# A pre-norm transformer layer on one core: row maxima split into parts with fewer VectorE operations, value copies on ScalarE, and the value bias folded into the output bias

## The chip, the cores and the metric

The kernel runs on one core of one Trainium2 chip. The metric is the device time of one execution in microseconds (us); 1381.62 us is the median of the three runs of the kernel before (1381.47, 1381.62 and 1383.63).

## The reference

The input is x of shape (2, 2048, 256) in fp32. It goes through attention with 16 heads of 16 columns, causal, with rotary positions, and then through a gated feed-forward layer whose inputs and weights are rounded to a 4-bit grid in blocks of 16. Cut to what matters here:

```python
q = split_heads(x @ Wq.T + bq)
k = split_heads(x @ Wk.T + bk)
v = split_heads(x @ Wv.T + bv)
q, k = (rope(q), rope(k))
att = jnp.einsum('bhqd,bhkd->bhqk', q, k) / scale
att = jax.nn.softmax(jnp.where(mask, att, -jnp.inf), axis=-1)
y = jnp.einsum('bhqk,bhkd->bhqd', att, v)
return y.transpose(0, 2, 1, 3).reshape(b, t, N_EMBD) @ Wo.T + bo
...
x = x + _L0_attn_ref(_layernorm(x), ...)
x = x + _L0_ffn_ref(_layernorm(x), ...)
```

The rows of `att` sum to one, so a constant bv that is added to every row of v comes out of the attention unchanged, and `Wo` turns it into the constant row `bv @ Wo.T`, which stands beside `bo`. The drawn bv and bo are not zero.

## The kernel before

**Tiles and stages.** Each of the two sequences has 2048 rows, which are cut into four chunks of 512 (c = 0 to 3). For a chunk the kernel normalizes x, turns it on TensorE (PE) into `xnT`, and makes queries, keys and values. The values of a chunk are computed in two pairs of 128-row tiles (`values`, L1011): eight matmuls fill one PSUM bank `pv` with 2 x 256 columns, and `put` (L1027) adds the bias and lays the result out in the tile `v`, 16 columns behind one column of ones for each head (so the same product also gives the softmax's denominators). The bias comes from `bvb`, bv on all 128 partitions, which SyncE's queue (SP) fetches by a broadcast transfer (L455).

The 16 heads are treated in four groups of four; a group of a chunk is a slot, and there are 2 x 4 x 4 = 32 slots. A slot has three steps:

- `max_steps` (L1075): PE computes the scores q.k into PSUM (`sc`, L1094, two banks at a time, masked on the diagonal at L1062), and VectorE (DVE) reduces each bank to its row maxima (`reduced`, L1106; instructions at L1118). For c = 0 a row has one part and the maxima are in `mx`; for c > 0 there is one partial maximum for each block of keys, in `parts`.
- `split` (L1137): the 16 maxima of each partition are written as a sum of three bf16 numbers, because PE's transpose carries bf16. For c > 0 a reduction (L1143) first makes `mx` of `parts`. Then, twice, a bitwise AND with `UPPER` (L1156) takes the upper 16 bits as a part, and a subtraction (L1159) leaves the rest. The parts lie in the tile `mslots`, 32 places for each of 16 maxima. `turn` (L1166) transposes the upper halves of `mslots` on PE (L1175), and ScalarE (ACT) copies them to `mT` (L1179).
- `value_steps` (L1203): PE computes the scores again with the maxima subtracted by a matmul with `less` (`sx`, L1227 and L1235), ACT takes the exponential (L1250), PE multiplies with `v` (`av`, L1283), and ACT copies the sums out (L1305).

Beside this run the feed-forward layer of an earlier chunk (`ffn_steps`: `pg` L1575, `pd` L1669, turned tiles `pth` L1434; its 4-bit rounding uses GpSimd (POOL) at L593, L615, L618 and L621 and DVE at L582 to L612), the rotary steps of the next chunk on POOL (L889, L892, L919), and transfers on SP. The row `bob` (bo on all partitions, L452) is added to x by POOL (L1503) before the output projection.

**What sets the order.** The program does not run its loops in the order in which they are written. Every piece of work is given to a planner (`Plan`, `add`) with its engine, a cost in microseconds, what it reads and writes, and a due time; a list scheduler (`ordered`) plays the plan through and emits each engine's instructions in the order that results. A changed cost or engine can therefore move other instructions too. `Thing` names a piece of data or a buffer, `ROOM` tells how many buffers of a kind there are, and seven PSUM banks (`ps`) are shared by all of it. Within the first 170 planned us, where the planner sees PE idle, `kept_busy` (L484) puts idle matmuls (L488) there. Each engine works through its own instructions strictly in order.

**Names of the change.** `bqk` (L445) holds the biases of queries and keys, turned by PE from the rows `brows` (`transpose_biases`). `bvb`, `UPPER` and the tile `left` are in the kernel before only. `on_vector(n)` and `on_scalar(n)` are the planner's costs for n columns.

Of the kernel before, what the change touches and what calls it, by code (L numbers as in the profile page):

```python
# [29 lines left out]
F32 = mybir.dt.float32  # L30
# [30 lines left out]
)  # L61
MAGIC = 1.5 * 2.0**22
EXPONENT = 0x7F800000
UPPER = -0x10000

# [27 lines left out]

XIN = 3
ROOM = dict(ps=7, av=1, ex=4, qT=4, parts=4)
ROOM.update(mx=2, mparts=1, left=1, mT=2, avs=1, den=2, y=2, sums=2, over=1)
ROOM.update(xnT=1, xin=XIN, high=1, t1=1, t2=1, cs=1, dev=XIN-1)
ROOM.update(x0=1, xT=1, x1=2, xn=2, h=1, hrT=1, step=1, fdev=2, sc16=2, sc44=2, endsc16=2, endsc44=2)  # L100

# [198 lines left out]
def product(n):  # L300

    return max(n / 600, 0.17 + n / 870, 0.23) + 0.005
# [12 lines left out]
def layer_kernel(  # L315
# [123 lines left out]
    mslots = const.tile([P, TPC, GROUP, SLOT], F32, name="mslots")  # L439

    slots_of = Thing()
    bvb_, bob_ = Thing(), Thing()


    bqk = const.tile([P, 2, NBLK], F32, name="bqk")  # L445
    brows = exps.tile([2 * NBLK, P], F32, tag="ex", name="brows")
    for i, vec in enumerate((bq, bk)):
        nc.scalar.dma_start(
            brows[i * NBLK : (i + 1) * NBLK], vec.rearrange("(n o) -> n o", n=NBLK)
        )  # L450
    bvb = const.tile([P, E], F32, name="bvb")
    bob = const.tile([P, E], F32, name="bob")  # L452

    def lay_bias(tile, vec, thing, due):
        run = lambda: nc.sync.dma_start(tile, vec.partition_broadcast(P))  # L455
# [331 lines left out]
    def project_steps(b, c, blk):  # L787
# [223 lines left out]
        def values(pair, due):  # L1011
            pm = Thing("ps")

            def run(n):
                if n == 0:
                    st["pv", pair] = small(CH, "pv").rearrange("p (i o) -> p i o", i=2)
                i = 2 * pair + n
                for k in range(KE):
                    nc.tensor.matmul(  # L1019
                        st["pv", pair][:, n, :],  # L1020
                        lhsT=xnTs[b, c][:, k, i * P : (i + 1) * P],
                        rhs=wvT[:, k, :],
                        start=(k == 0),
                        stop=(k == KE - 1),
                    )

            def put():  # L1027
                nc.vector.tensor_tensor(  # L1028
                    vs[b, c][:, : TPC * N_HEAD * AUG].rearrange(
                        "p (i h e) -> p i h e", i=TPC, e=AUG  # L1030
                    )[:, 2 * pair : 2 * pair + 2, :, 1:],
                    st["pv", pair].rearrange("p i (h e) -> p i h e", e=HD),
                    bvb.rearrange("p (h e) -> p h e", e=HD)
                    .unsqueeze(1)
                    .to_broadcast([P, 2, N_HEAD, HD]),
                    ALU.add,
                )

            for n in range(2):
                add(PE, KE * product(E), lambda n=n: run(n), [xnT_[b, c], wv_], [pm], due)  # L1040
            add(DVE, 0.595, put, [pm, bvb_], [v_[b, c]], due)

        if early:
            begin.stripped = stripped
# [30 lines left out]
    def max_steps(b, c, g):  # L1075

        steps = []
        st = {}
        mx, parts = Thing("mx"), Thing("mparts")
        found = []  # L1080
        max_[b, c, g] = Thing("mT")

        def one(i, kc, d, due):
            duo = 2 * (g % 2) + d
            cols = CH if kc < c else (i + 1) * P
            ps, got = (Thing("ps"), Thing("ps")), []

            def run():
                qT = qTs[b, c, g]
                kT = kTs[b, kc, g // 2]  # L1090
                sc = [ps_s.tile([P, CH], F32, tag="ps", name="sc") for _ in range(2)]
                kept_busy(sc[0])
                for h in range(2):
                    nc.tensor.matmul(  # L1094
                        sc[h][:, :cols],
                        lhsT=strips(qT, h, d, slice(i * P, (i + 1) * P)),
                        rhs=strips(kT, h, duo, slice(0, cols)),
                        start=True,
                        stop=(kc < c),
                    )  # L1100
                if kc == c:
                    for h in range(2):
                        masked(sc, h, cols - P, mask_q)
                got.append(sc)

            def reduced(h):  # L1106
                name = "parts" if c else "mx"
                if name not in st:
                    st[name] = att.tile(
                        [P, TPC, 2, 2, NC] if c else [P, TPC, 2, 2],  # L1110
                        F32,
                        tag=name,
                        name=name,
                        bufs=1 if c else 2,
                    )
                at = st[name][:, i, h, d]
                dst = at[:, kc : kc + 1] if c else at.unsqueeze(1)
                nc.vector.tensor_reduce(dst, got[0][h][:, :cols], AX.X, ALU.max)  # L1118

            add(  # L1120
                PE,
                0.18 + 0.44e-3 * cols if kc == c else 0.27,
                run,
                [qT_[b, c, g], k_[b, kc, g // 2][g % 2], mask_q_, pick_],
                [*ps, m_order],
                due,
                [parts if c else mx],
                "strip",
                FEED_M,
                0.07,  # L1130
            )
            for h in range(2):
                own = Thing(of=parts if c else mx)
                found.append(own)
                add(DVE, on_vector(cols), lambda h=h: reduced(h), [ps[h]], [own], due)

        def split(due):  # L1137
            left = Thing("left")

            def run():  # L1140
                if c:
                    st["mx"] = att.tile([P, TPC, 2, 2], F32, tag="mx", name="mx")
                    nc.vector.tensor_reduce(  # L1143
                        st["mx"].rearrange("p i h d -> p (i h d)"),
                        st["parts"][:, :, :, :, : c + 1].rearrange(
                            "p i h d k -> p (i h d) k"
                        ),
                        AX.X,
                        ALU.max,
                    )  # L1150

                mx = st["mx"].rearrange("p i h d -> p i (h d)")
                rest = att.tile([P, TPC, GROUP], F32, tag="left", name="left", bufs=1)
                for n, (src, rest) in enumerate(((mx, rest), (rest, mslots[:, :, :, 2]))):
                    part = mslots[:, :, :, n]
                    nc.vector.tensor_scalar(  # L1156
                        part.bitcast(I32), src.bitcast(I32), UPPER, None, ALU.bitwise_and
                    )
                    nc.vector.tensor_tensor(rest, src, part, ALU.subtract)  # L1159

            if c:
                add(DVE, 1.04, run, found, [mx, left, slots_of], due - 0.1)
            else:
                add(DVE, 0.79, run, found, [left, slots_of], due - 0.1)

        def turn(due):  # L1166
            pm = Thing("ps")

            def run():

                upper = mslots.bitcast(BF16).rearrange("p i s (d two) -> p i (s d) two", two=2)
                bank = ps_s.tile([P, TPC, P], BF16, tag="ps", name="ptm")
                st["pt"] = bank
                for i in range(TPC):
                    nc.tensor.transpose(st["pt"][:, i, :], upper[:, i, :, 1], ident_b)  # L1175

            def put():
                mT = att.tile([P, CH], BF16, tag="mT", name="mT")
                nc.scalar.copy(mT, st["pt"].rearrange("p i q -> p (i q)"))  # L1179
                maxima[b, c, g] = mT  # L1180

            add(
                PE,
                0.01 + 0.08 * TPC,
                run,
                [slots_of, ident_b_],
                [pm],
                due - 0.1,
                [max_[b, c, g]],
                late=0.05,  # L1190
            )
            add(ACT, on_scalar(CH), put, [pm], [max_[b, c, g]], due - 0.1)

        for i in range(TPC):
            for kc in range(c + 1):
                for d in range(2):
                    steps.append(lambda due, i=i, kc=kc, d=d: one(i, kc, d, due))
        return steps, split, turn
# [645 lines left out]
    def transpose_biases(due):  # L1844
        pm, got = Thing("ps"), []

        def run():
            got.append(small(2 * NBLK, "ptb"))
            nc.tensor.transpose(got[0], brows, ident[: 2 * NBLK, : 2 * NBLK])

        add(PE, 0.16, run, [biases, fixed], [pm], due)
        add(
# [7 lines left out]

    begun += [(-9.88, steps[0])]
    begun += [
        (-8.6, lambda due: lay_bias(bvb, bv, bvb_, due)),
        (0.4, lambda due: lay_bias(bob, bo, bob_, due)),
        (-8.8, lay_spread),
        (-8.2, lay_mask_q),
        (-8.1, lay_pick),
# [100 lines left out]
```

## Time and profile before

| What | Value |
|---|---|
| median of three timed runs | 1381.62 us |
| span of the profiled execution (first to last instruction) | 1378.9 us |
| what the median has beyond that span | 2.7 us |
| PE busy / DVE busy | 1317.6 us (96%) / 1115.1 us (81%) |
| ACT busy / POOL busy | 749.9 us (54%) / 538.4 us (39%) |
| instructions at L1156 (AND) | 64: 13.0 + 11.1 us busy |
| instructions at L1159 (subtract) | 64: 8.6 + 9.2 us busy |
| instructions at L1028 (values plus bias, DVE) | 16: 10.7 us busy |
| mean granted TensorE clock | 0.979 of full speed |

The profiled execution is not one of the three timed ones; its own time is known as its span. Busy time is the time in which an engine had an instruction running. A busy PE is not necessarily a PE at full speed, since the ends of matmuls are modelled. The chain that ended last is followed from the last instruction back: at each step to what released it, or to the instruction before it on its engine. PEld is PE's weight load, which waits for the buffers that its matmul needs.

### The profile page before, as it was taken

The page shows a single profiled execution, that of the slowest core. Times are in us where ns is not written, and L with a number is a line of the kernel's source. Part 1 is how long each engine was busy: PE and PEld are TensorE (multiplying, and loading weights), DVE is VectorE, ACT ScalarE, POOL GpSimd, SP SyncE. Part 2 cuts the span into 40 slices and gives each one's busy share as a digit, 9 for nine tenths or more (in the row PEclk, how much of TensorE's full clock was granted, in tenths as well). Part 3 has the DMA queues.
Part 4 walks back from the last instruction along what each step waited for, and adds up shares of the span by engine and source line. Part 5 has one row for each costly group of instructions (what it writes and reads, how often), then busy time and mean ns, then how long its engine had stood idle before and what let it go on. Part 6 is the DMA issues. An engine that isn't in the chain of part 4 may idle for free.

```text
span 1378.9 us, 27730 instructions
## 1 busy us (share of the span) xinstructions
PE 1317.6 (96%) x10408; PEld 656.7 (48%) x10408; DVE 1115.1 (81%) x2415; ACT 749.9 (54%) x1670; POOL 538.4 (39%) x685
## 2 busy tenths in 40 slices
PE   7988999999999999999998999999999999999977
PEld 4544444444544444444454555444454444444445
DVE  7788989988889998875479888996878988894296
ACT  2542655556555566557643455554655566667711
POOL 4754634434423334314345644432442332320360
PEclk8998999999999999999999999999999999999988
DMA  2653432411221401221343414240130130000000
GB/s 88 133 134 100 103 94 58 104 33 55 62 41 44 107 20 41 64 45 51 89 113 94 108 44 97 66 95 22 47 86 17 43 81 13 9 9 9 9 1 19
DMA packets 61887, 84.39 MB, mean 61 GB/s; under 512 B 14772, under 2 KB 30520, under 8 KB 61752
## 3 DMA queue, kind: packets, MB, share of 16 engines
q1 hardware_dynamic: 61744, 82.61, 24.2%
q8 instruction: 82, 1.34, 0.4%
q14 instruction: 53, 0.43, 0.1%
q10 hardware_dynamic: 8, 0.00, 0.0%
HBM read 55.09 MB, written 27.49 MB: 60 GB/s over the span
## 4 chain that ended last, share of the span: by engine, by line
PE 65%; DVE 19%; POOL 5%; issue 5%; DMA 3%; ACT 2%; SPq 0%; POOLq 0%; DVEq 0%; ACTq 0%
PE av L1283 15%; PE sc L1094 9%; PE pg L1575 9%; PE sx L1227 8%; DVE parts L1118 7%; PE sx L1235 7%; PE pd L1669 6%; PE pj L837 3%; PE pth L1434 2%; PE po L1519 1%; PE pv L1019 1%; DVE scale L582 1%; DVE step L609 1%; DVE mx L1118 1%; PE sc L1062 1%
## 5 line engine op out<-in xcount | busy, mean ns | idle before, releaser
L1250 ACT ACTIVATE ex<-sx 128x512 f32<-128x512 f32 (+3 forms) x1280 | 592.8, 538 | 345.9 <-PE sx L1235 202.1
L1118 DVE TENSOR_REDUCE parts<-sc 128x1 f32<-128x512 f32 (+3 forms) x1152 | 637.9, 611 | 65.2 <-PE sc L1094 46.6
L1235 PE MATMUL sx<-qT,kT 64*128 64x512 f32 (+3 forms) x1280 | 335.6, 521 | 0.0
L1283 PE MATMUL av<-ex,v 128*32 128x512 f32 (+3 forms) x2560 | 301.3, 543 | 0.0
L1094 PE MATMUL sc<-kT,qT 64*128 64x512 f32 (+3 forms) x1280 | 280.3, 425 | 8.9 <-DMA kT<-parts 2.5
L1227 PE MATMUL sx<-mT,less 64*128 64x512 bf16 (+3 forms) x1280 | 246.5, 355 | 5.4 <-DVE parts L1118 1.6
L1094 PEld LDWEIGHTS sc<-kT,qT 64*128 64x128 f32 x1280 | 132.8, 188 | 168.1 <-DVE parts L1118 51.2
L1227 PEld LDWEIGHTS <-less 64*128 64x128 bf16 x1280 | 66.5, 94 | 213.3 <-issue 205.5
L590 POOL TENSOR_SCALAR inv<-inv 128x16 f32<-128x16 f32 (+2 forms) x82 | 17.7, 216 | 373.0 <-DVE inv L586 341.2
L1235 PEld LDWEIGHTS sx<-qT,kT 64*128 64x128 f32 x1280 | 131.3, 196 | 9.0 <-issue 6.8
L1669 PE MATMUL pd<-wdT,hrT 128*128 128x256 f32 (+1 forms) x384 | 103.9, 411 | 1.5 <-ACT hrT L1438 1.0
L1283 PEld LDWEIGHTS av<-ex,v 128*32 128x32 f32 x2560 | 52.6, 108 | 70.8 <-issue 60.4
L1669 PEld LDWEIGHTS pd<-wdT,hrT 128*128 128x128 f32 (+1 forms) x384 | 70.4, 197 | 29.1 <-issue 16.0
L889 POOL TENSOR_TENSOR t<-t,cs 128x512 f32<-128x512 f32 x31 | 39.9, 1286 | 110.2 <-DVE t L883 104.8
L1575 PE MATMUL pg<-wgT,xT 128*128 128x352 f32 x224 | 76.9, 476 | 0.9 <-ACT xT L1438 0.8
L837 PE MATMUL pj<-xnT,wqkT 128*128 128x512 f32 x128 | 73.8, 672 | 3.5 <-DVE v L1028 1.7
L1118 DVE TENSOR_REDUCE mx<-sc 128x1 f32<-128x128 f32 (+3 forms) x128 | 54.3, 477 | 25.8 <-PE sc L1062 25.8
L1575 PE MATMUL pg<-wuT,xT 128*128 128x352 f32 x224 | 74.4, 471 | 0.1
L1062 PE MATMUL sc<-pick,mask_q 64*128 64x64 bf16 x1024 | 67.3, 198 | 0.0
L615 POOL TENSOR_TENSOR h<-h,step 128x704 f32<-128x704 f32 x28 | 47.2, 1686 | 48.8 <-DVE step L612 41.0
L1601 ACT ACTIVATE h<-pg 128x352 f32<-128x352 f32 x64 | 29.9, 467 | 64.6 <-PE pg L1575 56.5
L547 POOL TENSOR_SCALAR ve<-mv 128x1 f32<-128x1 f32 x64 | 12.6, 197 | 130.4 <-DVE mv L543 127.1
(163 smaller groups left out, 1614.8 us busy)
## 6 DMA issues: line engine op xcount, KB each, us to landing
qT<-parts SPq DMA_DIRECT2D x120, 128.0 KB
kT<-parts SPq DMA_DIRECT2D x120, 128.0 KB
parts<-high SPq DMA_DIRECT2D x30, 256.0 KB
parts<-t SPq DMA_DIRECT2D x30, 256.0 KB
sums<-avs SPq DMA_DIRECT2D x28, 256.0 KB
cs<-in_rope_dram SPq DMA_DIRECT2D x8, 512.0 KB
xin<-in_L_attn_x_dram SPq DMA_DIRECT2D x28, 128.0 KB
y<-sums SPq DMA_DIRECT2D x28, 128.0 KB
```

Source lines behind the costliest of these rows:

```text
L615: queue.tensor_tensor(src(), src(), st["step"], ALU.add)
L837: nc.tensor.matmul(got["pj"], lhsT=wqkT[:, k, i, cols], rhs=xnTs[b, c][:, k, :], start=(k == 0), stop=(k == KE - 1),)
L889: (nc.gpsimd if early and i == 0 else queue).tensor_tensor(swapped, swapped, angles[b, c][:, 1, :], ALU.mult)
L1062: nc.tensor.matmul(sc[h][:, col + at : col + at + STRIP], lhsT=strips(mask, h, half), rhs=strips(pick, h), start=False, stop=(half == 1),)
L1094: nc.tensor.matmul(sc[h][:, :cols], lhsT=strips(qT, h, d, slice(i * P, (i + 1) * P)), rhs=strips(kT, h, duo, slice(0, cols)), start=True, ...
L1118: nc.vector.tensor_reduce(dst, got[0][h][:, :cols], AX.X, ALU.max)
L1227: nc.tensor.matmul(sc[h][:, off:], lhsT=strips(less[d], h), rhs=strips(mT, h, slice(off, CH)), start=True, stop=False,)
L1235: nc.tensor.matmul(sc[h][:, off:], lhsT=strips(kT, h, duo, slice(jj, jj + P)), rhs=strips(qT, h, d, slice(off, CH)), start=False, stop=(j ...
L1250: nc.scalar.activation(st[j, d][:, h, off:], got[0][h][:, off:], AF.Exp, scale=HD**-0.5)
L1283: nc.tensor.matmul(st["av"][SLOT * s : SLOT * (s + 1), off:], lhsT=v[:, at : at + SLOT], rhs=st[j, d][:, h, off:], start=(j == 0), stop=(j ...
L1575: nc.tensor.matmul(got[half], lhsT=split("xrT")[:, k, :], rhs=wT[:, k, half * IH : (half + 1) * IH], start=(k == 0), stop=(k == KE - 1),)
L1669: nc.tensor.matmul(st["pd"], lhsT=st["hrT"][:n, k, :], rhs=wdT[:n, k, :], start=(k == 0), stop=(k == KI - 1),)
```

## The change

The split loses its ANDs: each subtraction reads the upper half of the number before it directly, as a bf16 view of `mslots`. For c > 0 the reduction of `parts` writes its result straight into the first place of `mslots`; for c = 0 a copy brings `mx` there. So a split has three DVE operations (reduction or copy, subtraction, subtraction) in place of five (c > 0) or four (c = 0). `mx` (for c > 0) and `left` are gone. Values are copied by ACT from PSUM to `v` without a bias. bv comes as two more rows of `brows` on ACT's queue, is turned with bq and bk, spread by two ACT copies to `wide`, multiplied with `woT` on PE, and added to `bob` by DVE (`through_output`, due at 2.0). The broadcast transfer of bv is gone. The costs given to the planner change with these steps.

```diff
-            left = Thing("left")
+            def upper(t):
+                return t.bitcast(BF16).rearrange("p i s (d two) -> p i s d two", two=2)[
+                    :, :, :, :, 1
+                ]

             def run():
+                first, second, third = (mslots[:, :, :, n] for n in range(3))
                 if c:
-                    st["mx"] = att.tile([P, TPC, 2, 2], F32, tag="mx", name="mx")
                     nc.vector.tensor_reduce(
-                        st["mx"].rearrange("p i h d -> p (i h d)"),
+                        first,
...
-                mx = st["mx"].rearrange("p i h d -> p i (h d)")
-                rest = att.tile([P, TPC, GROUP], F32, tag="left", name="left", bufs=1)
-                for n, (src, rest) in enumerate(((mx, rest), (rest, mslots[:, :, :, 2]))):
-                    part = mslots[:, :, :, n]
-                    nc.vector.tensor_scalar(
-                        part.bitcast(I32), src.bitcast(I32), UPPER, None, ALU.bitwise_and
-                    )
-                    nc.vector.tensor_tensor(rest, src, part, ALU.subtract)
-            if c:
-                add(DVE, 1.04, run, found, [mx, left, slots_of], due - 0.1)
-            else:
-                add(DVE, 0.79, run, found, [left, slots_of], due - 0.1)
+                else:
+                    nc.vector.tensor_copy(first, st["mx"].rearrange("p i h d -> p i (h d)"))
+                high = upper(mslots)
+                nc.vector.tensor_tensor(second, first, high[:, :, :, 0], ALU.subtract)
+                nc.vector.tensor_tensor(third, second, high[:, :, :, 1], ALU.subtract)
+            add(DVE, 0.72 if c else 0.6, run, found, [slots_of], due - 0.1)
```

```diff
             def put():
-                nc.vector.tensor_tensor(
+                nc.scalar.copy(
                     vs[b, c][:, : TPC * N_HEAD * AUG].rearrange(
                         "p (i h e) -> p i h e", i=TPC, e=AUG
                     )[:, 2 * pair : 2 * pair + 2, :, 1:],
                     st["pv", pair].rearrange("p i (h e) -> p i h e", e=HD),
-                    bvb.rearrange("p (h e) -> p h e", e=HD)
...
-                    ALU.add,
                 )
-            add(DVE, 0.595, put, [pm, bvb_], [v_[b, c]], due)
+            add(ACT, on_scalar(CH), put, [pm], [v_[b, c]], due)
```

```diff
-    for i, vec in enumerate((bq, bk)):
+    for i, vec in enumerate((bq, bk, bv)):
         nc.scalar.dma_start(
...
-    bvb = const.tile([P, E], F32, name="bvb")
+    def through_output(due):
+        temp, pm, st = Thing("x1"), Thing("ps"), {}
+        def spread_out():
+            st["wide"] = ffn.tile([P, E], F32, tag="x1", name="wide", bufs=ROOM["x1"]).rearrange(
+                "p (k o) -> p k o", k=KE
+            )
+            for k in range(KE):
+                nc.scalar.copy(st["wide"][:, k, :], bqk[:, 2, k : k + 1].to_broadcast([P, P]))
+        def run():
+            st["po"] = small(E, "pbo")
+            for k in range(KE):
+                nc.tensor.matmul(
+                    st["po"],
+                    lhsT=st["wide"][:, k, :],
+                    rhs=woT[:, k, :],
...
+        def put():
+            nc.vector.tensor_tensor(bob, st["po"], bob, ALU.add)
+        add(ACT, 0.4, spread_out, [bias_], [temp], due)
+        add(PE, KE * product(E), run, [temp, wo_], [pm], due)
+        add(DVE, on_vector(E), put, [pm], [bob_], due)
...
-        (-8.6, lambda due: lay_bias(bvb, bv, bvb_, due)),
         (0.4, lambda due: lay_bias(bob, bo, bob_, due)),
+        (2.0, through_output),
```

More of the change, by code (lines that the diff above doesn't have):

```diff
@@ L63 @@
 EXPONENT = 0x7F800000
-UPPER = -0x10000
 AHEAD = 3
@@ L97 @@
 ROOM = dict(ps=7, av=1, ex=4, qT=4, parts=4)
-ROOM.update(mx=2, mparts=1, left=1, mT=2, avs=1, den=2, y=2, sums=2, over=1)
+ROOM.update(mx=2, mparts=1, mT=2, avs=1, den=2, y=2, sums=2, over=1)
 ROOM.update(xnT=1, xin=XIN, high=1, t1=1, t2=1, cs=1, dev=XIN-1)
@@ L441, in layer_kernel @@
     slots_of = Thing()
-    bvb_, bob_ = Thing(), Thing()
-    bqk = const.tile([P, 2, NBLK], F32, name="bqk")
-    brows = exps.tile([2 * NBLK, P], F32, tag="ex", name="brows")
-    for i, vec in enumerate((bq, bk)):
+    bob_ = Thing()
+    bqk = const.tile([P, 3, NBLK], F32, name="bqk")
+    brows = exps.tile([3 * NBLK, P], F32, tag="ex", name="brows")
+    for i, vec in enumerate((bq, bk, bv)):
         nc.scalar.dma_start(
@@ L450, in layer_kernel @@
         )
-    bvb = const.tile([P, E], F32, name="bvb")
     bob = const.tile([P, E], F32, name="bob")
+    def through_output(due):
[13 more added lines that the diff above has]
+                    rhs=woT[:, k, :],
+                    start=(k == 0),
+                    stop=(k == KE - 1),
+                )
+        def put():
[3 more added lines that the diff above has]
+        add(DVE, on_vector(E), put, [pm], [bob_], due)
     def lay_bias(tile, vec, thing, due):
@@ L1032, in put @@
                     st["pv", pair].rearrange("p i (h e) -> p i h e", e=HD),
-                    bvb.rearrange("p (h e) -> p h e", e=HD)
-                    .unsqueeze(1)
-                    .to_broadcast([P, 2, N_HEAD, HD]),
-                    ALU.add,
                 )
@@ L1078, in max_steps @@
         st = {}
-        mx, parts = Thing("mx"), Thing("mparts")
+        whole = Thing("mparts" if c else "mx")
         found = []
@@ L1126, in one @@
                 due,
-                [parts if c else mx],
+                [whole],
                 "strip",
@@ L1132, in one @@
             for h in range(2):
-                own = Thing(of=parts if c else mx)
+                own = Thing(of=whole)
                 found.append(own)
@@ L1137, in split @@
         def split(due):
-            left = Thing("left")
+            def upper(t):
+                return t.bitcast(BF16).rearrange("p i s (d two) -> p i s d two", two=2)[
+                    :, :, :, :, 1
+                ]
             def run():
+                first, second, third = (mslots[:, :, :, n] for n in range(3))
                 if c:
-                    st["mx"] = att.tile([P, TPC, 2, 2], F32, tag="mx", name="mx")
                     nc.vector.tensor_reduce(
-                        st["mx"].rearrange("p i h d -> p (i h d)"),
+                        first,
                         st["parts"][:, :, :, :, : c + 1].rearrange(
-                            "p i h d k -> p (i h d) k"
+                            "p i h d k -> p i (h d) k"
                         ),
@@ L1847, in run @@
         def run():
-            got.append(small(2 * NBLK, "ptb"))
-            nc.tensor.transpose(got[0], brows, ident[: 2 * NBLK, : 2 * NBLK])
+            got.append(small(3 * NBLK, "ptb"))
+            nc.tensor.transpose(got[0], brows, ident[: 3 * NBLK, : 3 * NBLK])
         add(PE, 0.16, run, [biases, fixed], [pm], due)
```

## The prediction

> **What bounds the kernel now.** I read the busy times first, then the chain of work that ended last, then the stretches of time, then the waits. From the page:
>
> ```profile
> PE 1317.6 (96%) x10408; PEld 656.7 (48%) x10408; DVE 1115.1 (81%) x2415; ACT 749.9 (54%) x1670; POOL 538.4 (39%) x685
> ...
> PE 65%; DVE 19%; POOL 5%; issue 5%; DMA 3%; ACT 2%; SPq 0%; POOLq 0%; DVEq 0%; ACTq 0%
> ```
>
> PE is the bound on average: it is idle for 1378.9 - 1317.6 = 61.3 us. The chain runs through DVE for 19% of the span and through ACT for 2%, so work taken from DVE counts for more than work given to ACT. An average hides stages; the stretches (length, then busy time of PE, PEld, DVE, ACT, POOL, then PE's clock) show them:
>
> ```profile
> 0.00:50.00 50.00, 41.60 (x302) 24.86 (x302) 41.14 (x111) 18.95 (x42) 26.93 (x57) 0.90 0.35 100
> 400.00:450.00 50.00, 49.04 (x402) 23.02 (x401) 47.67 (x97) 28.52 (x63) 21.77 (x25) 1.00 0.17 49
> 1100.00:1300.00 200.00, 199.31 (x1626) 88.30 (x1622) 145.97 (x295) 135.52 (x290) 56.73 (x65) 1.00 0.08 21
> 1300.00:1379.00 79.00, 62.03 (x266) 41.05 (x262) 54.67 (x105) 14.53 (x43) 24.78 (x38) 0.91 0.04 12
> ```
>
> The start waits on DVE; around 400 DVE is 95% busy beside a full PE; from 1100 to 1300 PE alone is full and nothing done on DVE matters; the last 79 us hold no split and no values. What PE's loads wait for (total us, times, longest):
>
> ```profile
> PEld sc L1094 <- DVE parts L1118: 51.2, 83, 1.5
> PEld sc L1094 <- ACT ex L1250: 35.6, 65, 1.1
> ...
> PEld L1175 <- DVE mslots L1159: 6.0, 6, 2.9
> ...
> PEld pj L837 <- DVE v L1028: 1.8, 1, 1.8
> ```
>
> PE waits for PSUM banks that DVE's reductions hold, nearly as often for banks that exponentials hold, and rarely for a split itself. Sorting PE's own idle gaps by the engine that ended them (from the trace's waits) gives DVE 6.2 us before 100, 15.9 from 100 to 1300, 5.6 after; ACT 2.4, 7.8 and 2.5.
>
> **The split.** DVE's groups, each with count, busy us, mean ns:
>
> ```profile
> L1156 DVE TENSOR_SCALAR mslots<-mx 128x16 int32<-128x16 int32 x32 | 13.0, 406 | 1.0
> ...
> L1028 DVE TENSOR_TENSOR v<-pv,bvb 128x512 f32<-128x512 f32 x16 | 10.7, 671 | 4.5 <-PE pv L1019 4.4
> ...
> L1156 DVE TENSOR_SCALAR mslots<-left 128x16 int32<-128x16 int32 x32 | 11.1, 347 | 1.1
> ...
> L1159 DVE TENSOR_TENSOR mslots<-left,mslots 128x16 f32<-128x16 f32 x32 | 9.2, 288 | 1.1
> L1159 DVE TENSOR_TENSOR left<-mx,mslots 128x16 f32<-128x16 f32 x32 | 8.6, 268 | 1.1
> ```
>
> The median of each of these four small groups is 183 to 190 ns, so their means are lifted by a few long ones. One split in the order of time shows why (start, us, engine, line):
>
> ```profile
> 445.51 0.21 DVE L1143 TENSOR_REDUCE mx<-parts 128x16 f32<-128x64 f32 x1
> 445.74 1.67 POOL L615 TENSOR_TENSOR h<-h,step 128x704 f32<-128x704 f32 x1 [1.68 <-DVE mx L1143]
> 445.76 1.69 DVE L1156 TENSOR_SCALAR mslots<-mx 128x16 int32<-128x16 int32 x1
> ...
> 447.48 0.18 DVE L1159 TENSOR_TENSOR left<-mx,mslots 128x16 f32<-128x16 f32 x1
> 447.49 1.74 POOL L618 TENSOR_TENSOR h<-h,step 128x704 f32<-128x704 f32 x1
> ...
> 447.70 1.56 DVE L1156 TENSOR_SCALAR mslots<-left 128x16 int32<-128x16 int32 x1
> ```
>
> An AND that starts just behind a POOL instruction ends with it: 0.18 us of work take 1.69. The first subtraction got in 10 ns ahead of POOL's next instruction and took 0.18. Over all splits 16 of 64 ANDs are long, and 10 of 64 subtractions (one took 1.24 behind POOL's L892), each beside a POOL instruction. The reductions at L1143 stay under 0.23.
>
> *Removed.* 64 ANDs go and 8 copies (c = 0) come: 56 operations net. From one dependent small operation to the next it is 0.21 us (447.48 to 447.70), so DVE loses 56 x 0.21 = 11.8 us. Of the 64 ANDs, 23 lie on the chain, in 12 of the 32 splits; four of these splits are of c = 0 and get a copy. Net 19 x 0.21 = **4.0 us** of the chain.
>
> *Port stalls.* The 23 take 13.9 us of the chain; at 0.20 each they would take 4.6, so 9.3 are stalls behind POOL. What becomes of these is unknown, because no row shows a subtraction directly behind the reduction, or one with a 2-byte, strided input. Bounds: all 9.3 go (if the new subtractions never stall, as L1143 never does) or none (if they inherit the place and stall like the long L1159s); a gain beyond 9.3 isn't there, and a loss would need more long operations than before, where there are fewer in all. The nearest row is L1159, which does stall, so I take a quarter: **2.3 us**. The price of one unstalled subtraction I take as 0.19 (its median); the copy for c = 0 as an unstalled AND, 0.18, and its stalls as an AND's.
>
> The Trainium skill, "SBUF — State Buffer", section "Who interferes with whom", speaks against that quarter: by it a VectorE instruction with two SBUF inputs contends with a GpSimd instruction that reads SBUF, and a reduction never does, so both subtractions would still block. The long L1159s agree with it. By that rule the stalls' term would be nothing, and the forecast below 1378.3.
>
> *Waits.* The reduction or copy now writes `mslots` itself and so must wait for the four transposes of the slot before, where formerly only the AND behind it did. Those stand right behind the last split, and the next split is some 12 us or more away (36.1, 50.7, 84.2 at the start), so this is hidden; without that cover, the reductions queued behind on DVE would wait, and PE for their banks.
>
> **The values.** Sixteen operations of 0.671 us leave DVE (10.7 us) and come to ACT. The nearest row there is ACT's PSUM copy `avs` of 128x512 at 0.588: 16 x 0.588 = 9.4 us. Writing 16 of 17 columns is not shown on ACT; DVE's strided L1028 costs no more than its plain 128x512 rows (0.68), so I bound it by 0.588 and ACT's dearest 128x512 form, 0.69. On the chain L1028 stands three times (20.7, 74.4, 1017.7), **1.8 us**. At 74.4 it had lain 5.5 us behind a weight tile's transfer at the head of DVE's queue, while ACT was idle, and PE waited 1.7 us for the bank. What is late next there are the reductions of `sc`. On ACT the copy waits for `pv` in order, with exponentials queued behind it, and PE waits for their banks. The same waits took 4.4 us of DVE's idle time (3 times). In the 3 us after `pv` ends ACT is idle for 0.8 to 3.0 us in each of the sixteen places, and ACT is on the chain for about 3% of its work: 9.4 us cost **0.4 us**.
>
> The Trainium skill, "ScalarE: Activation LUTs", section "Rules for kernel authors", says to use VectorE for additions and the like, up to about three times faster in bf16. The rows here (fp32 from PSUM) say otherwise, 0.588 on ACT against 0.671. At three times 0.671, an estimate from that page, the copies would take 32 us of ACT and the forecast would end about 1 us higher.
>
> **The bias path.** Added once, in the first 50 us: two ACT copies (0.28 each by the 128x128 `hrT` copy) while ACT is idle 31 of 50 us; two matmuls of 128x256 (0.38 by `pv`) where idle matmuls stood; a DVE addition (0.41 by L1678), on the path because DVE is the busy engine: **0.4 us**. A third bias transfer costs ACT's queue 0.24; PE's first real work after it starts at 5.02, behind `mask_q`, which hides up to 2 us. SP saves an issue of 0.47. `bob` is first needed at 135.3.
>
> **Sum.** 4.0 + 2.3 + 1.8 - 0.4 - 0.4 = 7.3 us off the chain. What is late next takes some of it back: 35.6 of the 86.8 us that loads of `sc` wait end on ACT already. I take off a third: 4.9 us. The span goes from 1378.9 to 1374.0. The median has 2.7 us more than that span, which I leave as it is: **1376.7 us**.
>
> **Rivals.**
> - *Stalls vanish and nothing is late next*: 4.0 + 9.3 + 1.8 - 0.8 = 14.3 us, 1367.3. For it: reductions never stall. Against: L1159 does.
> - *Hidden by PE*: only PE's direct waits shrink: 1.7 at `pj`, and two waits of PE for a split (3.1 us) by 0.42 each; less the 0.8 added, that is 1.7 us, 1379.9. For it: PE 96% busy, only 22.1 us of idle ended by DVE before 1300. Against: the loads' waits of 51.2 us, which a modelled matmul partly covers.
> - *Slower: the value copies hold up the exponentials.* Each stands in ACT's order before exponentials whose banks PE needs. If all sixteen pass on in full, 9.4 us come against 5.1 without the ACT term: +4.3, 1385.9. It decides from 9 of 16 copies on (5.1 / 0.588). For it: loads wait 35.6 us for exponentials. Against: ACT's idle time at those places.
> - *Slower: another order.* In the built programs about 1,160 of PE's 12,085 instructions fall out of the common order, most in the second quarter, some 8 slots. PE's idle time from 100 to 1300 is 29.1 us, about 1 us a slot; as much again there is +8 against -4.9: 1384.7.
>
> **Chances.** Forecast 0.44 (its own range 1373 to 1379), stalls vanish 0.12, hidden 0.20, copies 0.13, order 0.11. The likeliest is 1376.7; the range from 1367 to 1386 takes in the rivals' ends, because the stalls' term alone is open by 9.3 us. A measurement of this kernel can tell about 0.2% (2.8 us) from no change: faster 0.44 + 0.12 = 0.56, same 0.20, slower 0.13 + 0.11 = 0.24.
>
> **What would show it.** DVE busy falls by 11.8 + 10.7 - 0.4 plus the saved stalls, to about 1090; ACT rises to about 760. Long subtractions beside L615 and L618 show inherited stalls. Fewer of PE's waits for L1118, with those for exponentials no larger, show the gain passed on; larger waits for L1250 around the value copies show the third rival, and idle gaps of PE between 300 and 600 the fourth. I am wrong if DVE falls as told and the span doesn't.

## The result and the profile after

The changed kernel takes 1397.86 us (median of four runs, 1394.78 to 1402.97) against 1382.62 of the kernel before beside it: 1.0101 times, 95% interval 1.0073 to 1.0129. It is slower, where the prediction had it faster, and lies outside the predicted range. The profiled execution has a span of 1401.2 us and a mean granted clock of 0.972.

The page of the changed kernel, busy times and the chain by engine:

```profile
PE 1327.3 (95%) x10406; PEld 663.4 (47%) x10406; DVE 1096.3 (78%) x2344; ACT 760.0 (54%) x1688; POOL 539.2 (38%) x685
...
PE 59%; DVE 22%; DMA 6%; issue 5%; POOL 4%; ACT 2%; SPq 1%; POOLq 0%; DVEq 0%; ACTq 0%
```

DVE lost 18.8 us of work (foretold was about 1090 us busy) and ACT took 10.1 (foretold was about 760). Yet PE's idle time rose from 61.3 to 1401.2 - 1327.3 = 73.9 us, and transfers have 6% of the chain in place of 3%. PE's busy time rose by 9.7 us too. That goes with the lower clock: 1317.6 x 0.979 / 0.972 gives 1327.1, an estimate. The profiled execution is the slowest of the four, at the lowest clock. The small operations, by group (count, busy us, mean ns):

```profile
L1181 DVE TENSOR_TENSOR mslots<-mslots 128x16 f32<-128x16 f32 x32 | 10.2, 320 | 1.1
L1055 ACT COPY v<-pv 128x512 f32<-128x512 f32 x16 | 9.5, 591 | 7.4 <-PE pv L1046 7.4
L1182 DVE TENSOR_TENSOR mslots<-mslots 128x16 f32<-128x16 f32 x32 | 8.2, 258 | 1.1
L1170 DVE TENSOR_REDUCE mslots<-parts 128x16 f32<-128x32 f32 (+2 forms) x24 | 4.7, 194 | 0.3
```

The value copy costs 591 ns (foretold 588). The subtractions inherit the ANDs' place behind POOL, as one split in the order of time shows (start, us, engine): the first starts 70 ns behind POOL's L642 and ends with it, and the second, which starts with POOL's next instruction at 267.35, is not held.

```profile
266.38 0.20 DVE L1170 TENSOR_REDUCE mslots<-parts 128x16 f32<-128x48 f32 x1
266.54 0.72 POOL L642 TENSOR_TENSOR xn<-xn,step 128x256 f32<-128x256 f32 x1 [2.87 <-DVE step L639]
266.61 0.70 DVE L1181 TENSOR_TENSOR mslots<-mslots 128x16 f32<-128x16 f32 x1
...
267.35 0.79 POOL L645 TENSOR_TENSOR xn<-xn,step 128x256 f32<-128x256 f32 x1
267.35 0.19 DVE L1182 TENSOR_TENSOR mslots<-mslots 128x16 f32<-128x16 f32 x1
```

What PE's loads wait for before `sc` is in all nearly what it was before (51.2 and 35.6 us), so these sums don't show the loss:

```profile
PEld sc L1117 <- DVE parts L1141: 48.7, 78, 1.5
PEld sc L1117 <- ACT ex L1270: 35.6, 60, 2.4
```

PE's own wait for reductions ahead of `sx` did grow, here first before, then after:

```profile
PE sx L1227 <- DVE parts L1118: 1.6, 3, 0.9
PE sx L1247 <- DVE parts L1141: 6.5, 9, 2.8
```

The stretches that were shown of before (length, busy time of PE, PEld, DVE, ACT, POOL, then PE's clock) don't hold the loss either. In the first PE has 2.2 us less, yet the second slot's transposes begin at 52.5 us, before they began at 53.3. Around 400 DVE has 3.1 us less to do, and PE's 49.1 of 50 us stay.

```profile
0.00:50.00 50.00, 39.39 (x292) 23.52 (x292) 40.55 (x107) 19.66 (x43) 27.21 (x57) 0.93 0.32 94
400.00:450.00 50.00, 49.12 (x390) 23.64 (x388) 44.53 (x91) 28.13 (x61) 14.45 (x16) 1.00 0.13 39
1100.00:1300.00 200.00, 199.36 (x1624) 91.23 (x1620) 159.40 (x318) 128.64 (x275) 50.27 (x59) 1.00 0.10 25
```

DVE's own waits differ most before `reciprocal(den)`, again first before, then after:

```profile
DVE den L1360 <- DMA den<-sums: 4.6, 4, 1.9
DVE den L1380 <- DMA den<-sums: 22.9, 7, 6.0
```

`den` holds the softmax denominators. They go out of SBUF (`sums<-avs`, SP's queue), come back in another layout (`den<-sums`, 8 KB), are inverted by DVE, and go out again. In the chain of the changed kernel in order of time (start, us), these round trips now stand among its longest pieces:

```profile
54.05 7.38 DMA sums<-avs
62.71 6.93 DMA kT<-parts
69.71 6.14 DMA sums<-den
77.25 5.43 DMA den<-sums
110.12 6.36 DMA den<-sums
...
278.37 9.60 DMA kT<-parts
287.99 4.76 DMA den<-sums
```

None of these instructions was edited. The question is thus whether the edited instructions cost the time, or the order in which the planner emits all the others.

### The profile page after: what moved, and what is told of

The parts are those of the page before. It is cut to its first block, busy times and chain, and to the rows that moved or that the text cites. A ratio compares the mean times of both kernels' runs of the same rounds, so it can differ in the third digit from the quotient of the medians.

```text
span 1401.2 us, 27682 instructions
## 1 busy us (share of the span) xinstructions
PE 1327.3 (95%) x10406; PEld 663.4 (47%) x10406; DVE 1096.3 (78%) x2344; ACT 760.0 (54%) x1688; POOL 539.2 (38%) x685
## 4 chain that ended last, share of the span: by engine, by line
PE 59%; DVE 22%; DMA 6%; issue 5%; POOL 4%; ACT 2%; SPq 1%; POOLq 0%; DVEq 0%; ACTq 0%
PE av L1303 13%; DVE parts L1141 10%; PE pg L1595 8%; PE sc L1117 8%; PE sx L1247 8%; PE sx L1255 7%; PE pd L1689 5%; PE pj L864 2%; PE pth L1454 2%; DMA den<-sums 2%; DVE step L639 1%; PE po L1539 1%; DVE step L636 1%; DVE scale L609 1%; DMA kT<-parts 1%
## 5 line engine op out<-in xcount | busy, mean ns | idle before, releaser
L1255 PE MATMUL sx<-qT,kT 64*128 64x512 f32 (+3 forms) x1280 | 340.8, 526 | 0.0
L1247 PE MATMUL sx<-mT,less 64*128 64x512 bf16 (+3 forms) x1280 | 252.4, 358 | 12.5 <-DVE parts L1141 6.5
L1255 PEld LDWEIGHTS sx<-qT,kT 64*128 64x128 f32 x1280 | 133.5, 197 | 12.3 <-issue 10.5
L1595 PE MATMUL pg<-wuT,xT 128*128 128x352 f32 x224 | 73.9, 470 | 0.1
L642 POOL TENSOR_TENSOR h<-h,step 128x704 f32<-128x704 f32 x28 | 47.2, 1686 | 53.9 <-DVE step L639 52.2
L1085 PE MATMUL sx<-pick,mask_k 64*128 64x64 bf16 x1024 | 63.8, 197 | 0.0
```

Of the source, the lines that this page charges most:

```text
L642: queue.tensor_tensor(src(), src(), st["step"], ALU.add)
L1085: nc.tensor.matmul(sc[h][:, col + at : col + at + STRIP], lhsT=strips(mask, h, half), rhs=strips(pick, h), start=False, stop=(half == 1),)
L1247: nc.tensor.matmul(sc[h][:, off:], lhsT=strips(less[d], h), rhs=strips(mT, h, slice(off, CH)), start=True, stop=False,)
L1255: nc.tensor.matmul(sc[h][:, off:], lhsT=strips(kT, h, duo, slice(jj, jj + P)), rhs=strips(qT, h, d, slice(off, CH)), start=False, stop=(j ...
L1595: nc.tensor.matmul(got[half], lhsT=split("xrT")[:, k, :], rhs=wT[:, k, half * IH : (half + 1) * IH], start=(k == 0), stop=(k == KE - 1),)
```

## Experiments: order or instructions

**Theory A**: the changed instructions save time, and the new order costs more than they save. **Rival**: the changed instructions cost it.

*e1*: every changed instruction, with the planner told before's tasks and costs, so that all others keep before's order (1.04/0.79 us for a split, the values planned as a DVE task and run on ACT, the bias product put behind a transpose that is there anyway).

> All of the changed instructions (three-operation split, value copies on ScalarE, bias through the output weights), but the planner gets the old costs and engines, so that all other instructions stand exactly in the order of the kernel before. Theory A (the new order costs the time, the instructions themselves save some): 1374 to 1379 us, DVE's idle time behind den back to about 5 us. Theory B (the instructions cost the time, the value copies before the exponentials above all): 1392 to 1400 us.

*e2*: the reverse, before's instructions in the changed kernel's order. The bias path is issued with a factor of zero.

> The instructions of the kernel before (five- or four-operation split, values plus bias on DVE, bv by a broadcast transfer), but planned with the costs and engines of the changed kernel, so that all other instructions stand in its order. The bias steps are issued too, with a factor of zero. Theory A: 1398 to 1406 us, slower than the changed kernel by about the 5 us that its instructions save. Theory B: 1380 to 1385 us.

*e4*: values and bias path only, split as before.

> Only the values and the bias path are changed, the split and its planner costs are those of before. The order of PE is nearly that of before. Theory A: 1377 to 1384 us. Theory B (value copies hold up the exponentials): 1390 to 1398 us.

*e5*: no instruction changed, only two numbers for the planner:

```diff
-                add(DVE, 1.04, run, found, [mx, left, slots_of], due - 0.1)
+                add(DVE, 0.72, run, found, [mx, left, slots_of], due - 0.1)
-                add(DVE, 0.79, run, found, [left, slots_of], due - 0.1)
+                add(DVE, 0.6, run, found, [left, slots_of], due - 0.1)
```

> No instruction of the kernel before is changed; only the two numbers that the planner takes for a split go from 1.04 and 0.79 to 0.72 and 0.60. Theory A, with the order that follows from the split's cost as the cause: 1395 to 1405 us. Theory B: within 3 us of 1382.

*f2*: the changed kernel with those two numbers put back (`1.04 if c else 0.79`), nothing else.

> The changed kernel with two numbers changed: the planner is told 1.04 and 0.79 us for a split as before, in place of 0.72 and 0.60. Every instruction stays as changed; the order comes out nearly as before (11,326 of 11,550 common TensorE instructions). If the planner's numbers alone cost the time: as the run with the old order, 1373 to 1380 us, 0.993 to 0.998 of before. If the change of the value copies in the plan (ScalarE in place of VectorE) costs something by itself, as the values-only run hints with its 0.999: 1379 to 1385, 0.998 to 1.001. If the changed instructions are at fault after all: above 1.004.

*f3* and *f4*: the kernel before with 0.96/0.74, and with 1.12/0.84.

> The kernel before, no instruction changed; the planner is told 0.96 and 0.74 us for a split in place of 1.04 and 0.79, a quarter of the way to the changed kernel's numbers. The order still changes much (10,284 of 11,550 in common). If the understated cost is what harms (theory C), a quarter of the loss or less: 1.000 to 1.003. If any new order is a draw that mostly loses against the one before (theory B): no relation to the size of the step, most likely 1.003 to 1.010, and the VectorE waits at den tell the bad draws from the good.

> The kernel before, no instruction changed; the planner is told 1.12 and 0.84 us for a split, a step of the same size the other way. The order stays close (11,404 of 11,550 in common). Theory C (only too low a cost harms): 0.996 to 1.001. Theory B: since the order is nearly the old one, 0.998 to 1.002 too; it tells apart only whether a replanned order that resembles the old one is safe.

| kernel | instructions | order | median us | ratio to before, 95% interval |
|---|---|---|---|---|
| e1 | changed | old | 1376.12 | 0.9945 (0.9922 to 0.9968) |
| f2 | changed | near the old | 1372.24 | 0.9927 (0.9901 to 0.9953) |
| e4 | values only | near the old | 1383.55 | 0.9993 (0.9969 to 1.0017) |
| f4 | before's | near the old | 1382.49 | 1.0001 (0.9982 to 1.0019) |
| after | changed | new | 1397.86 | 1.0101 (1.0073 to 1.0129) |
| e2 | before's | the same new one | 1398.99 | 1.0101 (1.0070 to 1.0131) |
| e5 | before's | another new one | 1398.38 | 1.0087 (1.0054 to 1.0121) |
| f3 | before's | another new one | 1396.37 | 1.0101 (1.0074 to 1.0128) |

The ratios compare means of the runs, so they differ a little from the quotients of the medians. Theory A holds on both sides: the instructions in the old order save 0.55%, the new order with the old instructions costs 1.0%, and two planner costs turn the one into the other. One expectation failed: e2 should have been some 5 us slower than the changed kernel and has the same ratio. So in the new order the instructions save nothing that shows, though with an interval of 0.3% on each side 5 us are not excluded. f2 beats both kernels. f3 shows that a small step in the cost is no safeguard: a quarter of the way re-plans the kernel much as the whole way does (10,284 of 11,550 unchanged PE instructions in common order) and costs as much.

## Experiments: what the parts are worth in the old order

*i1* is the kernel before with the new `run` of the split alone, *i2* with the values and the bias path alone; planner tasks and costs stay, so every other instruction keeps its place.

> The kernel before with the changed split alone (three VectorE operations in place of five or four); the values, the biases and the planner's tasks and costs stay, so every other instruction stays in the old order. The prediction had 11.8 us less on VectorE, 4.0 of it on the chain, and 0 to 9.3 us for stalls beside GpSimd, of which it took 2.3, and a third off the whole. If the split carries the gain of the run with both in the old order (0.9945): 0.993 to 0.997, 1373 to 1379 us. If the values carry it: 0.998 to 1.001.

> The kernel before with the value copies on ScalarE and the bias path alone, in the old order, split as before. The prediction had 1.8 us saved on the chain against 0.4 for ScalarE and 0.4 for the bias path. If the split carries the gain: 0.998 to 1.001. If the values carry it: 0.993 to 0.997. If the value copies hold up the exponentials: above 1.001.

i1: 1373.82 us, 0.9930 (0.9906 to 0.9954). i2: 1384.05 us, 1.0005 (0.9988 to 1.0022). The split carries the gain. Of the values no gain shows, but the interval, from 1.7 us saved to 3.0 lost, can't tell the forecast 1.0 us from nothing. i1's subtractions by group:

```profile
L1159 DVE TENSOR_TENSOR mslots<-mslots 128x16 f32<-128x16 f32 x32 | 14.3, 445 | 1.1
L1160 DVE TENSOR_TENSOR mslots<-mslots 128x16 f32<-128x16 f32 x32 | 7.9, 247 | 1.1
```

The median of one is 194 and 192 ns; 12 of the first and 2 of the second are over 250 ns. What these, and two long copies, take above the medians is 10.8 us; in the kernel before it was 18.2 (17 ANDs, where the prediction counted 16, and 10 subtractions). Each long one, before and in i1, starts while a POOL instruction on two tiles runs and ends within 55 ns of it. So the stalls didn't vanish, but fewer operations are there to be caught. On the chain the split's ANDs and subtractions stood with 20.9 us; in i1 its subtractions and copies stand with 6.6.

## Experiments: where in the order

With the changed instructions there are now two orders, the **low** one (splits at 0.72/0.60, the changed kernel) and the **high** one (1.04/0.79, f2), 1.0101 - 0.9927 = 1.74% or 24 us apart.

*f1*, against the waits for `den`: in the low order, each reciprocal is emitted 14 DVE tasks later, and the transfers that need it move behind it.

> The changed kernel, with one edit in the order alone: each of VectorE's 28 reciprocals of den is put 14 VectorE tasks later in the emitted list, and SyncE's transfers that need its result (sums<-den, over<-sums) move behind it. TensorE, ScalarE and GpSimd keep the changed kernel's order. Theory D (the new order costs its time by VectorE standing before a reciprocal whose 8 KB transfer has not landed, 22.9 us in the changed kernel against 4.6 before): the waits at the reciprocal fall to some 5 us, TensorE's idle time from 73.9 to about 62 us, the granted clock returns to 0.98, and the time is 1377 to 1387 us, 0.995 to 1.003 of before. Rival (the den wait is one symptom; what is late is the transfers and the work of TensorE itself, so what stands behind the reciprocal would wait elsewhere): 1392 to 1399 us, 1.006 or more. In between, the share that is gained back is the den wait's share.

1424.35 us, 1.0294 (1.0265 to 1.0324). As a remedy, D fails. DVE's wait for `den` is gone, and SP's queue waits in its place (total us, times, longest), for `sums<-den` behind the late reciprocal:

```profile
SPq L1394 <- DVE den L1418: 118.9, 22, 16.0
```

In the changed kernel this wait has 21.7 us:

```profile
SPq L1356 <- DVE den L1380: 21.7, 10, 5.2
```

SP works in order, so inputs, rotary tables and outputs stand behind it: DVE's wait for `xin` goes from 4.4 to 15.7 us. Because f1 puts this new wait in, it doesn't decide whether the old one was a cause.

*h1* and *h2* play the planner twice and exchange SP's queue between the two orders; *h7* and *h8* tell it one cost for the first five splits and the other for the rest.

> The changed kernel's instructions. The planner is played twice, with a split at 0.72/0.60 (the changed kernel's order, called the low order) and at 1.04/0.79 (the order of the run with the old split costs, the high order). TensorE, VectorE, ScalarE and GpSimd are emitted in the low order, and SyncE's transfers in the high order. Theory Q (the low order loses by the order of SyncE's queue: VectorE's wait for den and SyncE's wait for the reciprocal are two faces of it): most of the 25.6 us between the two orders comes back, 1372 to 1382 us, 0.993 to 1.000 of before. Rival K (the loss is in the order of the compute engines, and the queue only follows it): 1393 to 1403, at or above 1.008. Rival F (neither order is bad by itself, the two must fit each other): above 1.012, for this kernel and for the next.

> The reverse: the compute engines in the high order, SyncE's transfers in the low order. Theory Q: the loss comes with the queue, 1390 to 1402 us, at or above 1.006. Rival K: 1370 to 1378, about 0.993. Rival F: above 1.005, with the kernel before this one above 1.012.

> The changed kernel's instructions; the planner is told 1.04/0.79 us for the first 5 splits and 0.72/0.60 for the other 27. The order follows the high order through the first 140 us, and the changed kernel's behind them. By the times at which the slots begin, the changed kernel had lost 11.5 us against the high order at slot 5 and 14 more behind it: if the loss is local to the places, 1383 to 1390 us, 1.001 to 1.005 of before. If the head sets all of it (a late start that is never made good, with the rest following): 1370 to 1377. If the tail alone matters (the head's loss is idle time that is caught up): 1393 to 1399.

> The reverse: 0.72/0.60 us for the first 5 splits, 1.04/0.79 for the rest. If the loss is local: 1381 to 1387 us, 0.999 to 1.003 of before. If the head sets all of it: 1393 to 1399. If the tail alone matters: 1370 to 1377.

| kernel | engines' order | SP's order | median us | ratio, 95% interval |
|---|---|---|---|---|
| h1 | low | high | 1393.82 | 1.0087 (1.0070 to 1.0105) |
| h2 | high | low | 1403.89 | 1.0147 (1.0129 to 1.0166) |
| h7 | high for 5 slots, then low | with it | 1391.10 | 1.0066 (1.0044 to 1.0087) |
| h8 | low for 5 slots, then high | with it | 1382.26 | 0.9995 (0.9981 to 1.0009) |

SP's queue alone doesn't cure the low order (h1, as rival K had it), but a queue that doesn't fit costs the high order 2.2% (h2, against K). None of the three theories holds for both runs. Head and tail each cost something: the low head alone 0.68% (h8 against f2), the low tail alone 1.39% (h7 against f2). Together that is 2.07%, where both at once cost 1.74%, so within the intervals they add up. h8 lies in the range expected of a local loss, h7 a little above it. Where the time goes is read from the begin of each slot's transposes (`ptm`) in the profiled executions, as us behind f2:

| slot (f2, us) | after | h8 | h7 | h1 | h2 | j2 | j1 |
|---|---|---|---|---|---|---|---|
| 2 (82.8) | 7.6 | 6.4 | 3.2 | 5.8 | 3.5 | 1.6 | 4.8 |
| 4 (128.8) | 11.6 | 8.4 | 4.4 | 12.0 | 13.6 | 2.5 | 6.8 |
| 8 (261.2) | 10.7 | 10.7 | 3.6 | 12.5 | 14.2 | 2.3 | 5.2 |
| 9 (311.7) | 17.1 | 9.7 | 9.7 | 11.7 | 24.8 | 12.8 | 4.5 |
| 13 (506.8) | 27.6 | 9.7 | 18.9 | 23.7 | 29.1 | 12.8 | 14.4 |
| 15 (628.9) | 23.4 | 9.7 | 14.7 | 19.5 | 29.0 | 12.8 | 10.2 |
| 31 (1252.6) | 30.2 | 9.8 | 22.7 | 25.6 | 35.8 | 15.5 | 12.0 |

The last two columns, whose runs come below, also show how far one execution can be trusted. Up to slot 8, j1 has the changed kernel's instructions in its order, and is 5.5 us ahead of it; j2 has f2's, and is 2.3 us behind. Differences of some 5 us in the head are thus within the scatter of single executions. A step between two rows is firmer. h8's column is the plainest: 10.7 us are lost by slot 8, and 9.7 to 9.8 remain from slot 9 to the end, where PE is full. From slot 8 to 9 the low SP order loses 6.4 (after), 6.1 (h7) and 10.6 (h2), and the high one nothing (h8, h1). Here is SP's queue of the changed kernel at that place (start, us):

```profile
277.40 0.40 SPq L1344 DMA_DIRECT2D sums<-avs  x1
277.90 0.38 SPq L839 DMA_DIRECT2D cs<-in_rope_dram  x1
278.37 8.98 SPq L980 DMA_DIRECT2D kT<-parts  x8
287.99 0.56 SPq L1351 DMA_DIRECT2D den<-sums  x1
```

and DVE's queue:

```profile
292.77 0.25 DVE L1380 RECIPROCAL den<-den 128x16 f32<-128x16 f32 x1 [6.03 <-DMA den<-sums]
```

`den<-sums` stands behind eight kT transfers that take SP 8.98 us, where the planner counts 0.46 x 8 = 3.7. DVE comes to the reciprocal 6.03 us too early, and the reductions behind it wait. *j1* and *j2* exchange these four steps at this one place and move nothing else: j1 puts `den<-sums` and `y<-sums` ahead of `cs` and kT in the changed kernel, j2 puts them behind in f2.

> The changed kernel with one swap in SyncE's queue, at one of 28 places (the eighth reciprocal, which waited 6.03 us at 292.8): den<-sums and y<-sums stand ahead of cs and the eight kT transfers, directly behind sums<-avs. Nothing else is moved, on any engine. If the wait at this place is a cause: it falls to 2 us or less, the step from slot 8 to slot 9 is made some 6 us shorter (it was 6.4 us longer than in the high order), and the end comes 4 to 7 us earlier, 1.005 to 1.007 of before. If the time is lost again behind it, or kT then comes late: the wait is gone or moved, and the ratio stays at 1.009 to 1.012.

> The reverse in the kernel with the old split costs (0.9927): at the same one place cs and the eight kT transfers are put ahead of den<-sums and y<-sums, nothing else moved. If the order of these four transfers is a cause by itself: VectorE waits 5 to 12 us there, the slots behind begin 5 to 10 us later to the end, 0.996 to 1.000 of before. If not: 0.992 to 0.995.

j1: 1392.93 us, 1.0058 (1.0040 to 1.0077). j2: 1385.13 us, 1.0002 (0.9983 to 1.0021). The swap gives 0.43% back to the changed kernel (slot 8 to 9 is 7.1 us shorter) and takes 0.75% from f2 (10.5 us from slot 8 to 9, in its column above, kept to the end). j2's DVE at the place:

```profile
283.50 0.25 DVE L1404 RECIPROCAL den<-den 128x16 f32<-128x16 f32 x1 [11.45 <-DMA den<-sums]
```

and j1's SP queue:

```profile
271.96 0.40 SPq L1369 DMA_DIRECT2D sums<-avs  x1
276.63 0.56 SPq L1376 DMA_DIRECT2D den<-sums  x1
277.25 0.55 SPq L1388 DMA_DIRECT2D y<-sums  x1
277.85 0.58 SPq L864 DMA_DIRECT2D cs<-in_rope_dram  x1
278.47 6.77 SPq L1005 DMA_DIRECT2D kT<-parts  x8
```

SP now stands some 4 us for `sums<-avs` to land, and that costs less. So this one place is shown as a cause, in both directions. A wait there goes with a lower clock as well as with idle time: from 260 to 310 us PE's granted clock is 0.90 to 0.93 in the profiles with the long wait (after, h7, h2, j2), and 1.00 in those without it (before, f2, h1, h8, j1).

*g1* and *g2* tell the planner the measured figures (kT's `late=8` becomes 19.5; the landing of `den<-sums` gets 3.5 us more).

> The changed kernel; one number for the planner changed: the eight kT transfers of a chunk are told to occupy SyncE's queue for 9.0 us (0.46 x 19.5) in place of 3.7 (0.46 x 8); the profile shows 8.98 us. The order is a new one (10,650 common with the changed kernel, 10,182 with the high order). If the loss comes from that understated occupation (VectorE stands before den because den's transfer was put behind kT's): no den wait over 3 us behind the first 140 us, and 0.993 to 1.002 of before. If a new order is mostly a draw: 1.003 to 1.012.

> The changed kernel; one number for the planner changed: the 8 KB transfer den<-sums is told to land after 5.5 us in place of 2.0; the profile shows 5 to 7. The reciprocal is then planned later, and what it holds up too. If the understated landing is the cause: den waits under 8 us in all, and 0.993 to 1.002. If not: 1.003 to 1.012. The run with the reciprocal moved later in the finished order (1.029) differs in that SyncE's queue was not planned around it.

g1: 1392.38 us, 1.0074 (1.0048 to 1.0100). g2: 1400.04 us, 1.0136 (1.0108 to 1.0165). The waits for `den` fell to 9.3 and 3.1 us, as meant, and the time didn't follow. Each number makes another order; where these orders lose was not traced. The total of the `den` waits doesn't tell a bad order from a good one either, as the expectation for f3 had it: h8 has 14.3 us of them at 0.9995, e5 12.0 at 1.0087, g2 3.1 at 1.0136. A wait that is cured in the model is no proof of a better order.

**What stays open.** Of the 24 us between the orders, the one place accounts for 6 to 10 and the first five slots for 5 to 9 (the changed kernel against h7, h8 against f2). In these five slots no wait is shown as the cause. DVE waits 12.4 us for `den` between 50 and 140 us in the changed kernel and 2.1 in f2, but at slot 4 f1, without those waits, is 7.3 us behind f2, no better than j1 with them (6.8), and h1, with the other SP order, is 12.0 behind. The rest, from slot 9 on, was not taken apart. In the low engines' order it is 7.5 to 13.9 us in the table (after, h7, h1, j1), about half of it between slots 12 and 15, but h2, with the high engines' order, loses 11.0 us there too.

## Why the prediction was wrong, point by point

- **The bound** held: PE full, DVE next, and a loss in front of PE is kept to the end (h8, j2).
- **The split** held in kind and was sized too low. 4.0 + 2.3 us less a third had been forecast, some 4.2; i1 measures 0.70%, 9.7 us (6.4 to 13.0), with DVE's busy time 12.9 us lower than before (1102.2). Two terms were too cautious. The stalls fell by 18.2 - 10.8 = 7.4 us over all splits, so a quarter of those on the chain was too little. And nothing shows the third that was taken off for what is late next: in i1 `sc`'s loads wait for exponentials as before (35.7 us), and the gain passed on.
- **That subtractions stall** was right. The page "SBUF — State Buffer", section "Who interferes with whom", of the Trainium skill had it, and its rule agrees with 14 long ones of 64 in i1; the consequence that the prediction drew from it, a stalls' term of nothing, does not hold, because an operation that is no longer there can't stall.
- **The values** stay undecided: 1.8 - 0.4 - 0.4 had been forecast, and i2 measures 1.0005 (0.9988 to 1.0022) with DVE 8.5 us less busy. That excludes neither the 1.0 us nor nothing. The third rival in full, copies holding up exponentials, would cost i2 9.4 - 1.8 + 0.4 = 8.0 us and is refuted by the same run; the loads' wait for exponentials is 36.0 us there, 35.6 before.
- **The sum** of 4.9 us holds with the order held: e1 saves 7.6 us (4.4 to 10.8). In part that is luck, since the split alone has more than double its share.
- **The step that failed** is the price of "another order". The forecast's sum has no term for it; it stands as the fourth rival, with its 1,160 instructions out of the common order, and was given 0.11 and +8 us by spreading PE's mean idle time of 1 us a slot over 8 slots. Measured, the order costs 14 us with the old instructions (e2) and 22 to 24 with the new ones (the changed kernel against e1 and f2), two to three times as much. It isn't an even spread either: 6 to 10 us come from one place, where DVE stands before a transfer that is queued behind eight others (j1, j2). PE's mean idle time in the old order didn't tell what the new one meets. Nor was the place right: it was looked for between 300 and 600, and 7 to 12 us were lost before 140 and 6 more by 312. The wait that carries the one place was small in the profile before (4.6 us at `den` in all) and was not priced for an order in which it grows. The rest of the order's cost stays open.

## What to carry to other kernels

Where a planner emits the order, its costs are part of the kernel: count how many unchanged instructions change places before pricing the edited ones. Here each replanned order with about a tenth or more of PE's unchanged instructions out of place came out 0.7 to 1.4% slower than before, whatever the edit was worth, and those with up to 2% (f2, f4, e4) did not. But a small count is no safeguard: j2 moves four steps of SP's queue and none of PE's, and costs 0.75%. So keep the old costs first, measure the instructions in the old order, and only then re-plan. And where an engine that works in order stands before a round trip through memory, look at what lies ahead of that transfer in its queue, not only at the transfer.

## What the runs showed of the hardware

- **The granted clock differs between executions of the same program.** In 95 runs of the kernel before, on four chips and nearly as widely on each, it was 0.970 to 0.983, with spans from 1388.9 to 1373.2 us, about 0.83 us for each 0.001. The profiled execution of j1 had 0.982 and 1381.5 us, the lowest span of its twelve. A kernel's time is therefore taken from the medians above, and of a profile the steps from slot to slot rather than its end.
- **The clock is below full mostly in the head, and not by PE's busy share alone.** From 50 to 100 us the profiles of the kernels here show 0.76 to 0.93. In the changed kernel it is 0.76, below, with 43.1 of 50 us busy; before had 0.90 with 43.1 as well, and j1, with the changed kernel's instructions and order there, 0.86 with 42.4.

```profile
50.00:100.00 50.00, 43.08 (x336) 24.64 (x333) 25.06 (x77) 18.69 (x47) 24.35 (x35) 0.76 0.50 115
```

- **A small transfer is not always quick among others.** The 8 KB of `den<-sums` are on the changed kernel's chain five times, for 2.23 to 6.36 us from the begin of the issue, where the planner counts 0.46 + 2.03. The Trainium skill, "DMA: Bandwidth & Descriptors", section "Anatomy of one DMA — SWDGE (gpsimd) path", has about 2.0 us of fixed cost and next to nothing for so few bytes, for transfers that GpSimd issues; these are issued by SP and stand beside others. The shortest is near that figure, and the longest is three times as much.
